# Mixing three phases of a bidirectional scan stage in each step

## The chip, the cores and the metric

The kernel runs on one core of one Trainium2 chip. The metric is device time in microseconds of one execution, as the median of several runs. Beside it there is one profiled execution, with its own time and a span from its first to its last instruction. Lines of the source are named L1034 and so on, as the profile names them. PE is the matrix engine, DVE the vector engine, ACT the scalar engine, POOL is GpSimd, and SP is the queue that issues every DMA of this kernel.

## The reference, cut to what matters

Four residual layers follow one another on an image batch of 32 x 192 channels x 56 x 56, all in float32: an attention layer, a bidirectional recurrence, a shifted small convolution, and a long convolution done by Fourier transforms. Each takes the group norm of its input and adds its result to that input. The change lies in the second layer:

```python
xs = jnp.transpose(x.reshape(B, C, H * W), (0, 2, 1))       # x is the group norm here
k, v, r = xs @ Wk.T, xs @ Wv.T, xs @ Wr.T
x_fwd = wkv_scan(real_w, u, k, v)                            # forward in the token index
x_bwd = flip(wkv_scan(real_w, u, flip(k, 1), flip(v, 1)), 1) # and backward
h = jax.nn.sigmoid(r) * 0.5 * (x_fwd + x_bwd)
h = (h - mean(h)) * rsqrt(var(h) + LN_EPS) * ln_g + ln_b     # layer norm over the channels
out = h @ Wo.T                                               # added to the layer's input
```

One scan keeps two running sums with a decay, one of exp(k) v and one of exp(k), and gives at each token (sum with a bonus u for the token itself) / (the same for the denominator). Tokens are the 3136 pixels of an image. A backward sum at a token needs every later token's k and v, so the backward scan of an image can only start when the forward pass over that image has computed k and v for its last chunk.

## The kernel before, in words

`scan_pairs` takes the images in 16 pairs. Channels lie on partitions: a pair needs three tiles, two of 128 channels (one for each image) and one that holds the last 64 channels of both. The 3136 tokens are cut in NM = 4 chunks of MC = 784, so everything of a chunk is three tiles of 128 x 784 float32 (`t` = 0, 1, 2). Tiles 0 and 1 go through PE together (`pairs.outer`, L835 and L838), tile 2 by itself (`pairs.inner`, L845 and L848).

For each pair the kernel has, in this order in the source:

- the forward half, for chunk 0 to 3: load x, normalize it on ACT to a new tile `xn` (L1016), matmuls with Wk and Wv, exp of k on ACT to `ek` (L1064), `bv` = v times `ek` on DVE (L1069), then for each tile the function `scan`: two scans on DVE (L1034), each with two one-element copies on POOL that carry the running sum in and out (L1029, L1035), and a scalar_tensor_tensor each (L1036). ACT inverts the denominator by a logarithm and an exponential (L1041, L1042), DVE multiplies (L1076) to `y`. `ek`, `bv` and `y` of all four chunks stay in SBUF.
- `stats_for(p + 1)`: all four chunks of the next pair are loaded, measured by bn_stats (L961), and `norm` makes the group norm's scale, which takes two small groups of matmuls (L977, L978 and the helper's lines) with DVE and ACT work between.
- the backward half, for chunk 3 to 0: load x again and normalize it, matmul with Wr, the sigmoid as three ACT passes to `g` (L1095, L1099, L1100), the same `scan` in reverse, and y = (y + backward) times g (L1103 to L1105). At once, for the same chunk, the layer norm and projection: matmul with a centring matrix, squares on ACT to `sq` (L1115), the mean of the squares and the projection on PE, log and exp to `rd` (L1131, L1132), and on DVE rd times the projection (L1133), the residual add onto the loaded x (L1134), bn_stats of the result, and four stores to DRAM (L1138).
- the group norm of the result, whose scale the next layer uses, and a guard that looks at the largest values (`seen`, L1148).

The order on each engine is not that of the source: a scheduler places instructions by what is ready in its own model, and by which tile slots are free. Pools have a fixed number of slots for each name: 6 for `x`, 12 for `ek`, for `bv` and for `y`, 12 together for the working tiles (`xn`, `g`, `sq`, `rd`), 5 for the scans' `p` and `q`, and 4 PSUM tiles of two banks[...]. An instruction that needs a slot waits until the last reader of the slot's former tile is done. Each engine and SP's queue works off its own list in order.

Of the kernel before, what the change touches and what calls it, by code (L numbers as in the profile page):

```python
# [30 lines left out]
S = 56  # L31
# [820 lines left out]
def scan_pairs(ctx: ExitStack, tc: tile.TileContext, a, k, x1, x2, rs2, wogT, count):  # L852
# [9 lines left out]
    wp = ctx.enter_context(tc.tile_pool(name="s_w", bufs=12))  # L862
# [12 lines left out]
    def parts(t):  # L875
        return [t[:, h * HM : (h + 1) * HM] for h in range(2)]
# [76 lines left out]
    def load(p, m):  # L953
        xs = [wp.tile([128, MC], F32, name="x", tag="x", bufs=6) for _ in range(3)]
        for r, t, ap in views(p, m):
            nc.sync.dma_start(out=xs[t][r], in_=ap)
        return xs
# [5 lines left out]
    def new_stats(name):  # L963
        return sp.tile([128, 3, 2 * NM, 6], F32, name=name, tag=name)

    def norm(st):
# [5 lines left out]
        mean = sp.tile([128, 3], F32, name="mean", tag="mean")  # L972
        d = sp.tile([128, 3], F32, name="d", tag="d")
        for step in range(2):
# [12 lines left out]
            else:  # L987
                rs = sp.tile([128, 3], F32, name="rs", tag="rs")
# [4 lines left out]
        nb = sp.tile([128, 3], F32, name="nb", tag="nb")  # L993
# [3 lines left out]
    def stats_for(p):  # L997
        st = new_stats("st1")
        for m in range(NM):
            for t, x in enumerate(load(p, m)):  # L1000
                stats_of(st, m, t, x)
        return norm(st)

    nxt = stats_for(0)
    for p in range(NB // 2):
        _, rs, nb = nxt
        seen = sp.tile([128, 5, 3 * NM], F32, name="seen", tag="seen")
        ek = [[kp.tile([128, MC], F32, name="ek", tag="ek") for _ in range(3)] for _ in range(NM)]
        bv = [[kp.tile([128, MC], F32, name="bv", tag="bv") for _ in range(3)] for _ in range(NM)]
        y = [[kp.tile([128, MC], F32, name="y", tag="y") for _ in range(3)] for _ in range(NM)]  # L1010

        def normed(m, rs=rs, nb=nb, p=p):
            xs = load(p, m)
            xn = [wp.tile([128, MC], F32, name="xn", tag="t") for _ in range(3)]
            for t in range(3):
                nc.scalar.activation(xn[t], xs[t], AF.Identity, bias=nb[:, t : t + 1], scale=rs[:, t : t + 1])  # L1016
            return xs, [parts(t) for t in xn]

        def scan(m, t, carry, rev):

            b, e = bv[m][t], ek[m][t]
            c = eu[:, of(t)]
            got = []
            for i, src in enumerate((b, e)):
                s = wp.tile([128, MC + 1], F32, name="pq"[i], tag="pq", bufs=5)
                edge, last = (MC, 0) if rev else (0, MC)
                out, before = (s[:, 0:MC], s[:, 1:]) if rev else (s[:, 1:], s[:, 0:MC])
                at = carry[t][i]
                nc.gpsimd.tensor_copy(s[:, edge : edge + 1], at)  # L1029
                if rev:  # L1030
                    out, data = out[:, ::-1], src[:, ::-1]
                else:
                    data = src[:, :]
                nc.vector.tensor_tensor_scan(out, decay[:, of(t)].to_broadcast([128, MC]), data, at, ALU.mult, ALU.add)  # L1034
                nc.gpsimd.tensor_copy(at, s[:, last : last + 1])  # L1035
                nc.vector.scalar_tensor_tensor(before, src, c, before, ALU.mult, ALU.add)  # L1036
                got.append(before)
            return got

        def inverse(den, m, t, which, seen=seen):  # L1040
            nc.scalar.activation(den, den, AF.Ln)  # L1041
            nc.scalar.activation(den, den, AF.Exp, scale=-1.0, accum_out=seen[:, which, 3 * m + t : 3 * m + t + 1])  # L1042

        def start():
            carry = [[sp.tile([128, 1], F32, name=f"c{i}{t}", tag=f"c{i}{t}") for i in range(2)] for t in range(3)]
            for c in carry:
                for s in c:
                    nc.gpsimd.memset(s, 0.0)  # L1048
            return carry


        carry = start()
        for m in range(NM):
            _, xn = normed(m)
            for tiles in ((0, 1), (2,)):
                for wt in (wk, wv):
                    ps = [turned() for _ in tiles]
                    if len(tiles) == 2:
                        pairs.outer(wt, [s[2] for s in ps], xn)
                    else:  # L1060
                        pairs.inner(wt, ps[0][2], xn)
                    for t, (_, both, _) in zip(tiles, ps):
                        if wt is wk:
                            nc.scalar.activation(  # L1064
                                ek[m][t].rearrange("p (h n) -> p h n", h=2), both, AF.Exp,
                                accum_out=seen[:, 0, 3 * m + t : 3 * m + t + 1],
                            )
                        else:
                            nc.vector.tensor_tensor(  # L1069
                                bv[m][t].rearrange("p (h n) -> p h n", h=2), both,  # L1070
                                ek[m][t].rearrange("p (h n) -> p h n", h=2), ALU.mult,
                            )
                for t in tiles:
                    num, den = scan(m, t, carry, False)
                    inverse(den, m, t, 1)
                    nc.vector.tensor_tensor(y[m][t], num, den, ALU.mult)  # L1076

        if p + 1 < NB // 2:
            nxt = stats_for(p + 1)


        carry = start()
        st2 = new_stats("st2")
        for m in reversed(range(NM)):
            xs, xn = normed(m)
            h = y[m]
            for tiles in ((0, 1), (2,)):
                ps = [turned() for _ in tiles]
                if len(tiles) == 2:
                    pairs.outer(wr, [s[2] for s in ps], xn)  # L1090
                else:
                    pairs.inner(wr, ps[0][2], xn)
                for t, (_, both, _) in zip(tiles, ps):
                    g = wp.tile([128, MC], F32, name="g", tag="t")
                    nc.scalar.activation(  # L1095
                        g.rearrange("p (h n) -> p h n", h=2), both, AF.Exp, scale=-1.0,
                        accum_out=seen[:, 3, 3 * m + t : 3 * m + t + 1],
                    )
                    nc.scalar.activation(g, g, AF.Ln, bias=1.0)  # L1099
                    nc.scalar.activation(g, g, AF.Exp, scale=-1.0)  # L1100
                    num, den = scan(m, t, carry, True)
                    inverse(den, m, t, 2)
                    nc.vector.tensor_tensor(num, num, den, ALU.mult)  # L1103
                    nc.vector.tensor_tensor(h[t], h[t], num, ALU.add)
                    nc.vector.tensor_tensor(h[t], h[t], g, ALU.mult)  # L1105
            hs = [parts(t) for t in h]
            sq = [wp.tile([128, MC], F32, name="sq", tag="t") for _ in range(3)]
            for tiles in ((0, 1), (2,)):
                ps = [turned() for _ in tiles]
                if len(tiles) == 2:  # L1110
                    pairs.outer(centre, [s[2] for s in ps], hs)
                else:
                    pairs.inner(centre, ps[0][2], hs)
                for t, (_, both, _) in zip(tiles, ps):
                    nc.scalar.activation(  # L1115
                        sq[t].rearrange("p (h n) -> p h n", h=2), both, AF.Square,
                        accum_out=seen[:, 4, 3 * m + t : 3 * m + t + 1],
                    )
            sqs = [parts(t) for t in sq]
            for tiles in ((0, 1), (2,)):  # L1120
                pv, po = [turned() for _ in tiles], [turned() for _ in tiles]
                if len(tiles) == 2:
                    pairs.outer(mean_w, [s[2] for s in pv], sqs)
                    pairs.outer(wog, [s[2] for s in po], hs)
                else:
                    pairs.inner(mean_w, pv[0][2], sqs)
                    pairs.inner(wog, po[0][2], hs)
                for t, (_, var, _), (_, out, _) in zip(tiles, pv, po):
                    rd = wp.tile([128, MC], F32, name="rd", tag="t")
                    rdh = rd.rearrange("p (h n) -> p h n", h=2)  # L1130
# [6 lines left out]
            for r, t, i, c in places:  # L1137
                nc.sync.dma_start(out=x2[c, i, rows, p], in_=xs[t][r].rearrange("p (h w) -> p h w", w=S))  # L1138
# [567 lines left out]
```

## Time and profile before

| what | us |
|---|---|
| median of 3 runs (14577.73 to 14602.56) | 14596.81 |
| profiled execution, its own time | 14588.21 |
| its span | 14586.4 |
| scan stage within the span, 5402 to 9976 | 4574 |
| DVE busy in that stage | 3717.5 |
| PE busy in that stage | 3308.6 |
| ACT busy in that stage | 2132.1 |
| one pair, 5959.0 to 6240.5 | 281.5 |

The profile's first part gives the busy time of each engine over the whole span, in which the attention stage comes ahead of the scans (to about 5400) and the two convolutions behind them (from about 9976). Averages over the span therefore mix three stages. Busy time by stage, the list of who waited for whom, and the timeline of single instructions are asked for each stage apart. In a timeline line the first number is the start, the second the duration, and the bracket at the end gives the idle time of the engine just before, with the instruction that ended it.

### The profile page before, as it was taken

To read this page: it belongs to the slowest core of one execution; us is meant where nothing else is said; L and a number is where in the kernel's file an instruction comes from. 1 tells how busy PE (TensorE), PEld (TensorE's weight loads), DVE (VectorE), ACT (ScalarE), POOL (GpSimd) and SP (SyncE) were. 2 spreads that over 40 slices of the span, in tenths; PEclk is the share of its full clock that TensorE was granted. 3 is DMA by queue.
4 is the path that set the end of the run, shared out by engine and by line. 5 is a ranking of instruction groups with operands and counts; after the bars stand their busy time and mean duration, and the time that the engine had idled before them with its cause. 6 is when DMAs were issued, how large, how long until landed. Compare 5 with 4: busy or idle time off the path is not lost. (4 is left out here: it accounts for less than half of the span.)

```text
span 14586.4 us, 164705 instructions
## 1 busy us (share of the span) xinstructions
PE 12276.2 (84%) x63542; PEld 7620.1 (52%) x63542; DVE 11320.3 (78%) x15929; ACT 5972.2 (41%) x10826; POOL 2178.7 (15%) x2238
## 2 busy tenths in 40 slices
PE   4999999999999976777677677767899889988898
PEld 2655655655565553333333333335666666666666
DVE  4878877887887878878887887886777777777777
ACT  2444444444444434444444444443323232323323
POOL 0000000000000004434443443442000000000000
PEclk8999999999999988888888888888999999999999
DMA  2001001000100112232223222322111111111111
GB/s 54 27 27 40 27 27 40 27 27 32 35 27 27 40 53 66 60 71 71 65 67 81 66 60 68 75 51 56 35 37 36 37 37 36 37 35 38 36 37 23
DMA packets 886784, 654.14 MB, mean 45 GB/s; under 512 B 764942, under 2 KB 772857, under 8 KB 876976
## 3 DMA queue, kind: packets, MB, share of 16 engines
q1 hardware_dynamic: 885992, 643.51, 16.7%
q8 instruction: 505, 8.27, 0.2%
q14 instruction: 287, 2.35, 0.1%
HBM read 402.88 MB, written 240.50 MB: 44 GB/s over the span
## 5 line engine op out<-in xcount | busy, mean ns | idle before, releaser
L587 DVE SCALAR_TENSOR_TENSOR o<-v_a,dww,o 128x896 f32<-128x896 f32 (+1 forms) x1024 | 1052.8, 1028 | 390.1 <-ACT v_a L561 282.7
L1633 ACT COPY y<-ps 64x252 f32<-64x252 f32 (+1 forms) x2376 | 807.6, 340 | 1298.6 <-PE ps L1627 1266.4
L1567 PE MATMUL ps<-f,imag 84*84 84x112 f32 x6144 | 1032.0, 261 | 130.2 <-DVE imag L1560 128.5
L1574 ACT COPY z<-ps 84x448 f32<-84x448 f32 x768 | 405.3, 528 | 1771.1 <-PE ps L1567 1771.1
L1567 PE MATMUL ps<-f,real 84*84 84x112 f32 x6144 | 1035.7, 261 | 1.7
L1567 PEld LDWEIGHTS ps<-f,imag 84*84 84x84 f32 x6144 | 744.0, 153 | 275.6 <-DVE imag L1560 206.4
L1567 PEld LDWEIGHTS ps<-f,real 84*84 84x84 f32 x6144 | 748.8, 153 | 160.1 <-issue 68.6
L1041 ACT ACTIVATE q<-q 128x784 f32<-128x784 f32 x384 | 329.3, 858 | 1225.4 <-DVE q L1036 1223.9
L1035 POOL COPY c<-p 128x1 f32<-128x1 f32 x384 | 696.2, 1813 | 665.3 <-DVE p L1034 611.8
L1048 POOL MEMSET c<- 128x1 f32 x192 | 18.3, 99 | 5182.8 <-PE ps L719 5172.1
L1034 DVE TENSOR_TENSOR_SCAN q<-decay,c,ek 128x784 f32<-128x784 f32 x384 | 702.0, 1832 | 105.3 <-ACT ek L1064 105.2
L1583 PE MATMUL ps<-z,f 84*114 84x448 f32 x1536 | 658.5, 551 | 129.5 <-ACT z L1574 129.5
L604 ACT ACTIVATE pr<-ps,low 98x896 f32<-98x896 f32 (+1 forms) x384 | 350.1, 914 | 1015.4 <-DVE low L602 1015.4
L1585 DVE TENSOR_TENSOR o<-ps,rs 114x448 f32<-114x448 f32 x384 | 239.5, 624 | 631.7 <-PE ps L1583 630.5
L1035 POOL COPY c<-q 128x1 f32<-128x1 f32 x384 | 483.1, 1258 | 1460.7 <-DVE q L1034 1390.3
L1034 DVE TENSOR_TENSOR_SCAN p<-decay,c,bv 128x784 f32<-128x784 f32 x384 | 699.9, 1833 | 0.0
L674 PE MATMUL ps<-gq_a,xs_a 128*112 128x294 f32 x1792 | 643.7, 442 | 0.0
L600 PE MATMUL ps<-xs_a,gk_a 128*98 128x448 f32 (+1 forms) x1536 | 639.0, 497 | 0.0
L587 DVE SCALAR_TENSOR_TENSOR o<-v_c,dww,o 128x448 f32<-128x448 f32 (+1 forms) x1024 | 634.0, 619 | 4.0
L1547 PE MATMUL re<-y,f 128*84 128x420 f32 (+1 forms) x1152 | 561.5, 569 | 84.8 <-ACT y L1633 74.8
L601 PE MATMUL ps<-xs_c,gk_c 125*98 125x448 f32 (+1 forms) x1536 | 631.6, 492 | 0.0
L675 PE MATMUL ps<-gq_c,xs_c 125*112 125x294 f32 x1792 | 627.7, 433 | 0.0
(352 smaller groups left out, 29243.6 us busy)
## 6 DMA issues: line engine op xcount, KB each, us to landing
x<-x SPq DMA_DIRECT2D x512, 392.0 KB
x<-x SPq DMA_DIRECT2D x512, 196.0 KB
x<-x SPq DMA_DIRECT2D x192, 399.0 KB
out_x<-x SPq DMA_DIRECT2D x384, 196.0 KB
x_a<-in_x SPq DMA_DIRECT2D x32, 1568.0 KB
x<-x_a SPq DMA_DIRECT2D x32, 1568.0 KB
x_c<-in_x SPq DMA_DIRECT2D x64, 392.0 KB
x<-x_c SPq DMA_DIRECT2D x64, 392.0 KB
```

The costliest lines, as they stand in the source:

```text
L587: nc.vector.scalar_tensor_tensor(dst, tap(i), dww[:, t, i : i + 1], dst, ALU.mult, ALU.add)
L600: mm(ps[P2, h, :n], g[:, cols], xs_a[j][:, px], start=True, stop=False)
L601: mm(ps[P2, h, :n], gk_c[0:KC, 2 * j + h, cols], xs_c[j][0:KC, px], start=False, stop=True)
L674: mm(ps[:SUB, i, :HA], xs_a[j][:, px], g, start=True, stop=False)
L675: mm(ps[:SUB, i, :HA], xs_c[j][0:KC, px], gq_c[0:KC, 2 * j + (q + i) // ns], start=False, stop=True)
L1034: nc.vector.tensor_tensor_scan(out, decay[:, of(t)].to_broadcast([128, MC]), data, at, ALU.mult, ALU.add)
L1035: nc.gpsimd.tensor_copy(at, s[:, last : last + 1])
L1547: nc.tensor.matmul(ps[:, : n * 84], f2[:, i, :], y[:, i0 : i0 + n].rearrange("p g s u -> p (g s u)"), start=True, stop=True)
L1567: nc.tensor.matmul(ps[:84, i * 2 * S : (i + 1) * 2 * S], part[:, i0 + i].rearrange("p s u -> p (s u)"), f3[:, m, :], start=(m == 0), stop= ...
L1574: nc.scalar.copy(z[:, i0 : i0 + n].rearrange("p g m w -> p (g m w)"), ps[:84, : n * 2 * S])
L1583: nc.tensor.matmul(got, f4[:, m, :], z[:, i0 : i0 + n, m, :], start=(m == 0), stop=(m == 1))
L1633: nc.scalar.copy(y[64 * m : 64 * m + 64, 2 * g0 + i : 2 * (g0 + n) : 2], got[64 * i : 64 * i + 64, :, :, m, :])
```

## The change

The phases become functions, and the loop over pairs is written anew. A pair's data go into a `State`. `forwards(s, m)` is a chunk of the forward half and `backwards(s, m)` the backward sums of a chunk up to y times g. `finish(s, m)` is what came behind them in the same chunk: layer norm, projection, residual, stores. `measure` is the statistics of one chunk, `conclude` the group norm of the result and the guard.

Step i of pair p now holds: backwards of chunk 3 - i of pair p; finish of the chunk that the step before did (in step 0 this is chunk 0 of pair p - 1); forwards of chunk i of pair p + 1; in steps 0 and 1 the measuring of two chunks of pair p + 2; behind step 2 their norm; behind step 1 the group norm of pair p - 1's result. The statistics of pairs 0 and 1 and the forward half of pair 0 come ahead of the loop, the last finish behind it.

`normed` writes the normalized x over the loaded x, and `finish` loads x once more for the residual. Slots: `x` 7 in place of 6, working tiles 8 in place of 12 (no `xn` any more), `y` 16 in place of 12, and 3 or 4 for some small tiles. The decisive parts of the diff:

```diff
-    wp = ctx.enter_context(tc.tile_pool(name="s_w", bufs=12))
+    wp = ctx.enter_context(tc.tile_pool(name="s_w", bufs=8))
...
-        xs = [wp.tile([128, MC], F32, name="x", tag="x", bufs=6) for _ in range(3)]
+        xs = [wp.tile([128, MC], F32, name="x", tag="x", bufs=7) for _ in range(3)]
...
-            xs = load(p, m)
-            xn = [wp.tile([128, MC], F32, name="xn", tag="t") for _ in range(3)]
-            for t in range(3):
-                nc.scalar.activation(xn[t], xs[t], AF.Identity, bias=nb[:, t : t + 1], scale=rs[:, t : t + 1])
-            return xs, [parts(t) for t in xn]
+    def normed(s, m):
+        xs = load(s.p, m)
+        for t in range(3):
+            nc.scalar.activation(xs[t], xs[t], AF.Identity, bias=s.nb[:, t : t + 1], scale=s.rs[:, t : t + 1])
+        return [parts(t) for t in xs]
...
+        s.y[m] = [kp.tile([128, MC], F32, name="y", tag="y", bufs=3 * NM + 4) for _ in range(3)]
...
+    def finish(s, m):
+        h, xs = s.y[m], load(s.p, m)
...
-        if p + 1 < NB // 2:
-            nxt = stats_for(p + 1)
...
+    last = NB // 2
+
+    def measure(st, p, m):
+        for t, x in enumerate(load(p, m)):
+            stats_of(st, m, t, x)
+
+    s, after, before = State(0, norm(stats_for(0))), norm(stats_for(1)), None
+    for m in range(NM):
+        forwards(s, m)
+    for p in range(last):
+        ahead = State(p + 1, after) if p + 1 < last else None
+        st = new_stats("st1")
+        for i in range(NM):
+            m = NM - 1 - i
+            backwards(s, m)
+            if i > 0:
+                finish(s, m + 1)
+            elif before is not None:
+                finish(before, 0)
+            if ahead is not None:
+                forwards(ahead, i)
+            if p + 2 < last:
+                if i < 2:
+                    measure(st, p + 2, 2 * i)
+                    measure(st, p + 2, 2 * i + 1)
+                elif i == 2:
+                    after = norm(st)
+            if i == 1 and before is not None:
+                conclude(before)
+        before, s = s, ahead
+    finish(before, 0)
+    conclude(before)
```

The bodies of `forwards`, `backwards`, `finish` and `conclude` are those of the old halves, with the names of the `State`.

## The prediction

> **What bounds the kernel now.** I read the page first, then the busy time by stage, then VectorE's (DVE's) waits in the scan stage, then the timelines around a pair's end.
>
> ```profile
> PE 12276.2 (84%) x63542; PEld 7620.1 (52%) x63542; DVE 11320.3 (78%) x15929; ACT 5972.2 (41%) x10826; POOL 2178.7 (15%) x2238
> ```
>
> ```profile
> 5402.00:9976.00 4574.00, 3308.57 (x11650) 1537.11 (x11650) 3717.54 (x4170) 2132.06 (x3523) 1850.51 (x1712) 0.84 0.28 68
> 5959.00:6240.50 281.50, 205.86 (x722) 95.63 (x723) 229.56 (x257) 132.04 (x219) 116.00 (x108) 0.84 0.27 68
> ```
>
> The first is the page's line of the whole span; below it the scan stage and one pair of it (busy us of PE, PEld, DVE, ACT, POOL, then PE's clock, the DMA share, GB/s). The page would name PE as the bound; in this stage it is DVE, 229.6 of 281.5 us a pair, and nothing else passes 206. So 52 us a pair are DVE's gaps. Its waits in the stage:
>
> ```profile
> DVE rd L1133 <- PE ps L838: 340.8, 32, 14.7
> DVE y L1105 <- ACT g L1100: 166.4, 64, 5.1
> DVE q L1034 <- ACT ek L1064: 105.2, 16, 8.9
> DVE seen L1148 <- ACT sq L1115: 99.8, 16, 6.9
> DVE rs L989 <- PE ps L848: 85.4, 32, 3.1
> ```
>
> Columns: us in total, times, longest. The counts say where: 16 is once a pair. The forward half waits only for its first `ek`; the rest lies in the backward half and at the pair's end. One such end:
>
> ```profile
> 5964.48 1.86 DVE L1105 TENSOR_TENSOR y<-y,g 128x784 f32<-128x784 f32 x2 [5.13 <-ACT g L1100]
> 5967.80 0.98 DVE L1105 TENSOR_TENSOR y<-y,g 128x784 f32<-128x784 f32 x1 [1.38 <-ACT g L1100]
> 5974.40 0.17 DVE L1148 TENSOR_SCALAR seen<-seen 128x12 f32<-128x12 f32 x1 [5.62 <-ACT sq L1115]
> 5982.20 1.85 DVE L1133 TENSOR_TENSOR rd<-ps,rd 128x784 f32<-128x784 f32 x2 [7.38 <-PE ps L838]
> 5993.22 0.16 DVE L981 COPY mean<-ps 128x2 f32<-128x2 f32 x1 [1.52 <-PE ps L848]
> 5997.25 0.16 DVE L989 TENSOR_SCALAR rs<-ps 128x2 f32<-128x2 f32 x1 [3.11 <-PE ps L848]
> 5997.98 0.16 DVE L994 SCALAR_TENSOR_TENSOR nb<-mean,rs 128x3 f32<-128x3 f32 x1 [0.51 <-ACT rs L992]
> 6004.58 3.59 DVE L1034 TENSOR_TENSOR_SCAN q<-decay,c,ek 128x784 f32<-128x784 f32 x2 [6.31 <-ACT ek L1064]
> ```
>
> The brackets add to 31.0 us of idle in one pass: last chunk's layer norm, group norm, first `ek` of the next pair, one after another with no scan to fill them.
>
> **What the skill says.** "Perfetto Trace Analysis" (Optimization Strategy) advises interleaving regimes whose most-contended engine differs; the counts above agree that there is something to interleave. "PSUM — Partial Sum Buffer" (Engine vs sequencer instructions): the ACT, DVE and POOL queues are strict first-in-first-out, and matmuls start in program order; so a mixed order can still wait behind a late instruction. "TensorE: Matmul & The Clock Gate" (What's actually happening): PE falls to half clock after about 3.4 us idle and needs as long to recover. The trace agrees in kind:
>
> ```profile
> 6111.72 0.56 PE L977 MATMUL ps<-d,grp_aa 128*128 128x1 f32 x2 [5.22 <-DVE d L985]
> ...
> 6114.57 5.59 PE L835 MATMUL ps<-xn,Wr_aa 128*128 128x392 f32 x8
> 6120.09 1.91 PE L838 MATMUL ps<-xn,Wr_ca 64*128 64x392 f32 x8
> ```
>
> From `d` the group-norm matmuls take 2.85 us and the pair of Wr tiles 7.4, where warm ones (mean_aa 2.90, mean_ca 1.59) take 4.5.
>
> **The parts, costed.** Nothing is removed from DVE, ACT, PE or POOL; added are one load of x per chunk and nothing else. Loads go from 12 to 16 tile triples a pair: 14.4 MB to 19.3, with the stores' 4.8 some 24 MB in 256 us = 94 GB/s. At the stage's start the same loads ran at 256 GB/s, so bandwidth is covered; 16 more issues at 0.33 us on SP are 5 us a pair, hidden.
>
> *DVE's step.* From timeline start-to-start distances a scan takes 1.75 us, a scalar_tensor_tensor 0.94, a tensor_tensor 0.88, a bn_stats 0.47. Backward of a chunk (6 scans, 6 stt, 9 tt) is 24.1 us, finish (3 tt, 3 stt, 6 bn) 8.4, forward (6, 6, 6) 21.5: 54.0 a step, 216 a pair, plus 24 bn of measuring (11.4) and small ones: 229, the busy time above. That is the floor.
>
> *What still waits.* The built order of the changed program shows, per engine, the sequence below; I followed each of a pair's four steps through the in-order queues, with durations of the profile (ACT: ln 0.75, exp with sum 0.84, g or sq 0.80, x norm 0.93; PE: a pair of tiles 4.5 warm, a third tile 3.1). Zero is the first backward scan.
>
> Step 0 (chunk 3, finish of the predecessor's chunk 0): wog is done at 20.2, DVE comes to `rd` at 25.0: no wait. Step 1: wog 24.5, DVE 26.9: none; one bn_stats waits 0.7 for an x tile whose slot a store has to leave.
>
> Step 2: the group norm of the finished pair stands on PE ahead of Wr. `d` leaves DVE at 3.3, matmuls to 6.3 (DVE waits 1.4 at `rs`), Wr pair cold to 13.7. ACT then runs g, the q inverses and g's log and exp without a gap from 13.8 to 24.0, and only then sq. From sq to the pair of `rd` is mean 4.5 + wog 4.5: 33.9. DVE, with its backward done, arrives at 27.5: **6.4 us** wait, and 0.7 for the third tile.
>
> Then the new wait. In steps 2 and 3 the x norm of the next backward stands on ACT ahead of `ek`, and its load needs the slot of the tile that finish has just stored. The store and the reuse of its slot, the load and its reader:
>
> ```profile
> 6733.11 1.32 SPq L1138 DMA_DIRECT2D x<-x  x2
> 6737.08 0.33 SPq L956 DMA_DIRECT2D x<-x  x1
> ...
> 6842.02 1.85 SPq L956 DMA_DIRECT2D x<-x  x1
> ...
> 6847.20 1.04 ACT L1016 ACTIVATE xn<-x,nb,rs 128x784 f32<-128x784 f32 x1 [2.59 <-DMA x<-x]
> ```
>
> Store to slot 3.4 to 4.0 us, load 3.3 after its issue ends (about 2.9 by the fit in "DMA: Bandwidth & Descriptors", Anatomy of one DMA; that fit is for another issuing path, and I use the trace's number). So 7.2 from the end of the first residual add, norm 0.9, `ek` 0.9: 9.0, plus a hop. DVE's cover is the rest of finish, 5.6 us, and PE's Wk pair comes in at about the same time: DVE waits **2.8** before the forward scan. Behind that norm on ACT stand `ek` and the q inverses; who waits is only DVE's scan. The loads behind the stores on SP are for the later backward half and land in time.
>
> Step 3: the measuring norm, likewise: `d` at 5.6, `rs` wait 2.0, inverse waits 0.5; ACT takes g only after the second q logarithm (17.4), sq ends 29.2, PE gives wog at 36.6, DVE arrives at 28.5: **8.1**; third tile 0.6; `ek` 2.7.
>
> Sum: 0.7 + 11.3 + 13.9 = 26 us a pair in place of 52; a pair is 229.5 + 26 = 256. An extreme of 0 is DVE alone; an extreme of all of the old 14.7-us chain in every step is rival C.
>
> *POOL.* The edge copies stay in their number. In the old trace DVE never waits for POOL; in the new order each edge copy stands at least one scan ahead of its reader. I take 0; if a slot of the five p/q tiles comes late, 1.8 us (one copy, L1035) a step, 7 a pair.
>
> *Ends.* Statistics of pair 1 now stand ahead of the first scan: 12 more tiles at about 1.5 us (5405 to 5422 in the old trace for 12), partly instead of later work and with the first `ek` behind it: +14. Before, first scan (5437.8) to the last group norm (9964) is 4526. After: forward of pair 0 alone 89; 15 pairs of 256 = 3840, less 8.4 (no predecessor) and 11.4 (no pair to measure); pair 15 without a forward 130 busy + about 27 idle; its last finish 35 (chain 14.7, 8.4, norm 12). Sum 4101. Change: 4101 + 14 - 4526 = **-411 us**. On the profiled execution's 14588.2 that is 14177; on the median shown, 14596.8, it is **14186**.
>
> **Rivals.**
> A: DVE packs almost fully, idle 8 a pair: ACT or PE run ahead more than my walk allows. For it: the four PSUM tiles and ACT's 47% load leave room. Against: the sq-after-g order is fixed in the queue. 14186 - 15 x 18 = 13916.
> B: the chain is late in steps 0 and 1 too, where my slack is 5 and 2.4 us, through semaphore hops or cold matmuls: idle 43. 14186 + 15 x 17 = 14441.
> C, slower: the in-order queues reproduce the old worst wait at `rd` (14.7 us, as in the second fence's longest) in each of four steps, with norms 3.4 and `ek` 5.5 beside it: idle 68, 14186 + 15 x 42 = 14816. It decides from 53 us a pair, 13 a step, since 411/15 = 27 above my 26. Against it: finish works on the chunk of the step before, so its centre matmuls need nothing of the current scans; for it: nothing but the FIFO rule.
> That the change does not mix is excluded: in the built order every pair's forward scans stand between the predecessor's backward ones.
>
> **Numbers.** Forecast 0.55, A 0.17, B 0.19, C 0.07, about the same (no difference that counts) 0.02. The forecast's own range is idle 17 to 35 a pair: 14050 to 14320. For 8 in 10 I go into A and B: 13950 (idle 10) to 14440 (idle 43). Below 0.2% of the time, 29 us, this kernel's measurement does not tell a change. Faster 0.91, same 0.02, slower 0.07.
>
> **What would show it.** Right: DVE about 90% busy in the middle of the stage; `seen` and most `y` waits gone; waits of `rd` about twice a pair at 6 to 8 us; `rs` twice a pair at 1 to 2; and the forward q scan's wait for `ek` twice a pair near 3, with ACT's x norm waiting for DMA just before it. PE's clock above 0.84. Wrong: DVE waiting for POOL, or for DMA at bn_stats by more than 1 us; `rd` waits four times a pair; a gap in the first 100 us much above 14.

## The result, and the profile after

The changed kernel takes 14180.4 us (median of 4 runs, 14167.8 to 14187.8), the kernel before in the same session 14593.2 (14577.7 to 14602.6). The ratio is 0.9716, 95% interval 0.9704 to 0.9728: faster by 2.8%, 413 us. The forecast was 14186. Its profiled execution took 14187.84 us, with a span of 14185.5.

The page's line of the whole span, changed kernel (busy us, share, instructions):

```profile
PE 12164.8 (86%) x63542; PEld 7571.3 (53%) x63542; DVE 11327.6 (80%) x15929; ACT 5948.9 (42%) x10826; POOL 2153.5 (15%) x2238
```

The instruction counts of all engines and DVE's busy time (11320.3 before) are what they were. The span is shorter, and PE is busy 111 us less for the same instructions. The busy time by stretch (same columns as before: length; PE, PEld, DVE, ACT, POOL; PE's clock, DMA share, GB/s): 13 whole pairs of the changed kernel, then 13 whole pairs of the kernel before. A pair is counted from one `fine` mark to the next; that instruction ends the guard and comes once a pair.

```profile
5815.94:9172.24 3356.30, 2582.45 (x9460) 1204.46 (x9456) 3019.80 (x3367) 1711.34 (x2860) 1469.04 (x1398) 0.87 0.38 94
5693.02:9387.62 3694.60, 2689.59 (x9465) 1249.20 (x9465) 3015.70 (x3367) 1731.89 (x2860) 1499.99 (x1404) 0.84 0.28 69
```

A pair takes 258.2 us, of which DVE is busy 232.3 and idle 25.9; before, it took 284.2, with DVE busy 232.0 and idle 52.2. (The single pair shown for the kernel before, 281.5 with DVE busy 229.6, is a little shorter than this mean.) PE's clock stands at 0.87, 0.84 before.

What DVE waits for in the stage now (us in total, times, longest):

```profile
DVE rd L1132 <- PE ps L838: 197.8, 30, 10.8
DVE q L1035 <- ACT ek L1066: 96.3, 30, 8.3
DVE rs L989 <- PE ps L848: 60.6, 32, 3.1
```

`y <- g` (166.4 before) and `seen <- sq` (99.8 before) are gone but for one wait each. `rd` is down from 340.8 to 197.8, about twice a pair. `ek` now counts twice a pair where it was once. One pair on DVE's timeline, steps 2 and 3; in brackets the idle time ahead of each instruction and who ended it:

```profile
6956.94 0.16 DVE L989 TENSOR_SCALAR rs<-ps 128x2 f32<-128x2 f32 x1 [1.35 <-PE ps L848]
6983.84 1.86 DVE L1132 TENSOR_TENSOR rd<-ps,rd 128x784 f32<-128x784 f32 x2 [5.85 <-PE ps L838]
...
6996.56 3.59 DVE L1035 TENSOR_TENSOR_SCAN q<-decay,f,ek 128x784 f32<-128x784 f32 x2 [3.63 <-ACT ek L1066]
7025.98 0.16 DVE L989 TENSOR_SCALAR rs<-ps 128x2 f32<-128x2 f32 x1 [2.16 <-PE ps L848]
7053.35 1.86 DVE L1132 TENSOR_TENSOR rd<-ps,rd 128x784 f32<-128x784 f32 x2 [7.37 <-PE ps L838]
...
7065.40 3.60 DVE L1035 TENSOR_TENSOR_SCAN q<-decay,f,ek 128x784 f32<-128x784 f32 x2 [2.96 <-ACT ek L1066]
```

Nearly all that is left lies in steps 2 and 3, the steps behind a group norm. PE's timeline of step 2 shows what stands ahead of `rd` there:

```profile
6953.97 0.56 PE L977 MATMUL ps<-d,grp_aa 128*128 128x1 f32 x2 [18.16 <-DVE d L985]
...
6956.82 5.59 PE L835 MATMUL ps<-x,Wr_aa 128*128 128x392 f32 x8
...
6966.84 2.90 PE L835 MATMUL ps<-y,cen_aa 128*128 128x392 f32 x8
...
6974.97 2.90 PE L835 MATMUL ps<-sq,mean_aa 128*128 128x392 f32 x8 [0.73 <-ACT sq L1114]
...
6982.15 1.59 PE L838 MATMUL ps<-y,wog_ca 64*128 64x392 f32 x8
```

PE stands still for 18.16 us in front of the group norm's second half, because DVE comes to `d` only behind its forward scans. Wr and the centre matmuls (`cen`) are queued behind it, then the mean of the squares and the projection (`wog`). From `d` on PE runs almost without a gap: 30 us to `rd`, and DVE has only 22.7 us of other work in that time. By the Trainium skill ("PSUM — Partial Sum Buffer", Engine vs sequencer instructions) matmuls start in program order, and the trace agrees. How long the norm alone holds Wr is another question, since Wr also needs the last normalized x tile. The two steps differ in that, step 2 first:

```profile
6954.29 1.04 ACT L1017 ACTIVATE x<-x,nb,rs 128x784 f32<-128x784 f32 x1 [5.56 <-DMA x<-x]
```

```profile
7010.03 1.04 ACT L1017 ACTIVATE x<-x,nb,rs 128x784 f32<-128x784 f32 x1 [3.76 <-DMA x<-x]
7023.02 0.56 PE L977 MATMUL ps<-d,grp_aa 128*128 128x1 f32 x2 [16.89 <-DVE d L985]
7025.87 5.20 PE L835 MATMUL ps<-x,Wr_aa 128*128 128x392 f32 x8
```

In step 3 that tile is ready at 7011.1 and Wr starts at 7025.9: the norm holds Wr for 14.8 us. In step 2 the tile waits for its load and is ready at 6955.3, only 1.5 us before Wr starts; there the load is nearly as late as the norm.

The first Wr group is cold, 5.59 us for eight records where the warm centre group takes 2.90; that agrees with the skill's "TensorE: Matmul & The Clock Gate" (What's actually happening), since 18 us of idle went before it. That page has about 3.4 us for the way back to the full clock; here the eight records are slow for 5.5 us, after 2.85 us of the norm's own matmuls.

The second kind of wait on the timelines of ACT and of SP, the end of step 2:

```profile
6994.69 1.04 ACT L1017 ACTIVATE x<-x,nb,rs 128x784 f32<-128x784 f32 x1 [6.12 <-DMA x<-x]
6995.64 0.80 ACT L1066 ACTIVATE ek<-ps 128x784 f32<-128x784 f32 x1
```

```profile
6986.66 1.32 SPq L1137 DMA_DIRECT2D x<-x  x2
6990.64 0.33 SPq L956 DMA_DIRECT2D x<-x  x1
```

The two stores of tile 0 go out at 6986.66. The load for the next backward half has to wait for that slot, 3.98 us, and then lands 4.05 us after its issue, where ACT's x norm waits for it; `ek` stands behind that norm, and DVE's forward scan behind `ek`.

### The profile page after: what moved, and what is told of

Its sections match the earlier page's. It is cut to its first block, busy times and chain, and to the rows that moved or that the text cites. A ratio compares the mean times of both kernels' runs of the same rounds, so it can differ in the third digit from the quotient of the medians.

```text
span 14185.5 us, 165124 instructions
## 1 busy us (share of the span) xinstructions
PE 12164.8 (86%) x63542; PEld 7571.3 (53%) x63542; DVE 11327.6 (80%) x15929; ACT 5948.9 (42%) x10826; POOL 2153.5 (15%) x2238
## 5 line engine op out<-in xcount | busy, mean ns | idle before, releaser
L1480 POOL TENSOR_TENSOR mat<-tap,tap 114x114 f32<-114x114 f32 x96 | 40.9, 426 | 3790.9 <-PE ps L1538 2256.7
L1591 DVE TENSOR_TENSOR a<-re,g 84x420 f32<-84x420 f32 (+1 forms) x576 | 353.7, 614 | 245.2 <-PE re L1584 245.2
L1584 PE MATMUL im<-y,f 128*84 128x420 f32 (+1 forms) x1152 | 528.1, 540 | 0.0
L1664 PE MATMUL ps<-f,padded 114*128 114x168 f32 x3168 | 517.9, 319 | 11.4 <-issue 7.8
```

What stands on the lines that cost most here:

```text
L1584: nc.tensor.matmul(ps[:, : n * 84], f2[:, i, :], y[:, i0 : i0 + n].rearrange("p g s u -> p (g s u)"), start=True, stop=True)
L1591: nc.vector.tensor_tensor(a0, f[0], gr.to_broadcast(shape), ALU.mult)
L1664: nc.tensor.matmul(ps[:, g * 168 : (g + 1) * 168], flat[:, (g0 + g) * 128 : (g0 + g + 1) * 128], f1, start=True, stop=True)
```

## The experiments

They come in three groups: the reasons for the 25.9 us that are left; which half of the change brings the gain; the price of the added load, with checks on the readings before. The table sums them up. Each ratio is to runs of the kernel before beside it, whose medians lay between 14599.1 and 14600.0. "Idle" is DVE's idle time between 6100 and 9000 us of each kernel's profile, 2900 us in the middle of the stage (stretches that aren't whole pairs, so good to some us a pair).

| kernel | median us | ratio to before, 95% | DVE idle in 2900 us |
|---|---|---|---|
| before | 14599.8 | 1 | 526 |
| changed kernel, again | 14180.7 | 0.9713 (0.9700–0.9726) | 286 |
| group norms spread | 14081.4 | 0.9645 (0.9632–0.9658) | 221 |
| nine x tiles | 14122.1 | 0.9676 (0.9663–0.9690) | 256 |
| both | 14008.3 | 0.9592 (0.9578–0.9605) | 171 |
| mixed, layer norm in its own step | 14829.4 | 1.0166 (1.0149–1.0183) | 616 |
| not mixed, layer norm one step late | 14184.2 | 0.9724 (0.9708–0.9741) | 295 |
| changed, sq first | 14132.5 | 0.9689 (0.9672–0.9705) | 265 |
| all edits | 13864.3 | 0.9498 (0.9482–0.9514) | 60 |
| before, second load alone | 14581.1 | 0.9989 (0.9982–0.9995) | 515 |
| measuring in steps 2 and 3 | 14131.0 | 0.9679 (0.9663–0.9695) | 259 |
| not mixed, sq first, nine x tiles | 14247.8 | 0.9760 (0.9744–0.9777) | 336 |
| mixed, sq first, nine x tiles | 14106.7 | 0.9662 (0.9646–0.9678) | 238 |

### Why the rest is idle

The changed kernel itself, as the base:

> The changed kernel itself, as the base for the three variants beside it: 14180 us on the medians so far, within 0.2%; in the scan stage about 7 us of `rd` wait twice a pair, 1.3 to 2.2 us of `rs` wait twice a pair, about 3.2 us of `ek` wait twice a pair.

It came at 14180.7, so the three beside it can be set against it.

**The norms out of Wr's way.** `norm` becomes a generator, and `forwards` takes its parts at fixed places:

```diff
+    def norm_parts(st):
         ...
+        yield
         for step in range(2):
             ...
             pairs.inner(group, [ps[:, 1, 2:3]], [[s] for s in src])
+            yield
         ...
+        yield
         nc.vector.scalar_tensor_tensor(nb, mean, -1.0, rs, ALU.mult, ALU.mult)
+        yield mean, rs, nb
     ...
+    def forwards(s, m, side=None):
         ...
         for tiles in ((0, 1), (2,)):
+            if side is not None and len(tiles) == 2:
+                next(side)
             for wt in (wk, wv):
                 ...
+            if side is not None:
+                next(side)
             for t in tiles:
                 ...
+        return None if side is None else next(side)
```

So bn_aggr comes ahead of Wk, the means' matmuls behind Wv of tiles 0 and 1, `d` and its matmuls behind Wv of tile 2; a further `next` in `scan`, behind the first sum of tile 2, takes `rs`. The norms are the same two, in the same steps.

> Both group norms are spread through the forward half of their step instead of standing at its end, so that their matmuls on PE come before and just behind the third tile's Wv and no longer hold Wr until DVE has reached `d`. My theory (the norm ahead of Wr is what makes `rs` and `rd` late): the `rs` waits go (3.5 us a pair). In step 3 the Wr pair could start at the end of the last x norm, some 13 us earlier, so its `rd` wait of 7.4 goes too. In step 2 that x norm itself waits for its load (it ended at 6955.2 where Wr started at 6956.8), so only 1 to 2 of 5.9 us go there. About 12 us a pair, 14 pairs: 170 us less than the changed kernel, 14010. Rival (`rd` is late because ACT takes sq only behind all of g and the q inverses, and those wait for DVE's scans, wherever Wr starts): only the `rs` waits go, 50 us, 14130, and `rd` still waits 5 to 7 us in both steps.

Measured: 14081.4, 99 us less than the changed kernel, between the two. DVE's waits in the 2900 us:

```profile
DVE rs L994 <- PE ps L848: 51.9, 24, 2.2
DVE rd L1145 <- PE ps L838: 36.0, 11, 3.9
```

In the same stretch of the changed kernel `rd` had 140.0 us in 22 waits. Of two `rd` waits a pair one is gone, and the other fell from 7.37 to 3.87 us. In step 3, where the norm alone held Wr, moving it took 3.5 us off the wait. In step 2 the cause is not separated: the edit moved the load too. The last x norm ahead of Wr now ends 9.7 us before Wr starts, where it was 1.5, and by the trace of the changed kernel Wr could have started only those 1.5 us earlier with the norm alone out of its way. (Nine x tiles alone, the next run, leave both waits, 5.68 and 7.37 us.) Two things came otherwise than I expected. It is step 2's wait that went and step 3's that stayed, not the other way. And `rs` was not helped: each still waits 2.2 us, since the built order put it one instruction behind `d`, and PE's group norm takes that long from `d` wherever it stands.

**More x tiles.**

```diff
-    wp = ctx.enter_context(tc.tile_pool(name="s_w", bufs=8))
+    wp = ctx.enter_context(tc.tile_pool(name="s_w", bufs=6))
-        xs = [wp.tile([128, MC], F32, name="x", tag="x", bufs=7) for _ in range(3)]
+        xs = [wp.tile([128, MC], F32, name="x", tag="x", bufs=9) for _ in range(3)]
```

> Nine x tiles in place of seven (paid for with six instead of eight work tiles), so that the load for the next backward half no longer needs the slot of a tile that finish has just stored. My theory (store, slot, load, x norm on ACT ahead of `ek`): the `ek` waits of 3.6 and 3.0 us shrink by what the x norm is later than PE's Wk pair, 1.5 us or more each, at most to nothing: 3 to 6 us a pair, 14090 to 14135. Rival (PE's Wk pair is as late as the x norm, because it stands behind the wog that made `rd` late): `ek` still waits 3 us twice a pair and the time is that of the changed kernel, 14180, within 0.1%. In both, `rd` and `rs` stay as they are.

Measured: 14122.1, 59 us less. ACT's `ek` is now released by PE:

```profile
6972.47 0.82 ACT L1066 ACTIVATE ek<-ps 128x784 f32<-128x784 f32 x1 [5.51 <-PE ps L838]
```

```profile
DVE q L1035 <- ACT ek L1066: 46.1, 22, 2.1
```

No wait of `ek` is longer than 2.1 now, where they were 3.63 and 2.96. The waits of bn_stats for DMA (9.8 us in this stretch) are gone too. So both theories were partly right: the chain from store to load to x norm set the last 0.9 to 1.5 us of each wait, and behind it Wk, which PE takes behind the late wog, sets the other 2.1.

**Both edits.**

> Both edits together. My theory: with the norms out of Wr's way and the load for the next backward half no longer behind measuring or a store, Wr starts early in both steps, and all of 26 us of waits a pair but some 4 to 8 go: 20 us a pair, 14 pairs, 280 us: 13900, not below 13860 (DVE alone without waits). Rival (the ACT queue's order bounds `rd`): 14080 to 14130, with `rd` still at 5 to 7 us twice a pair.

Measured: 14008.3, between my number and the rival's, and 172 us less than the changed kernel; the two gains (99 and 59) add, and perhaps a little more. What is left:

```profile
DVE rs L994 <- PE ps L848: 52.0, 24, 2.2
DVE q L1041 <- ACT ek L1076: 49.8, 24, 2.1
DVE rd L1145 <- PE ps L838: 49.2, 21, 3.9
```

`rd` waits 2.3 us on average; here ACT's order shows at last: the third tile's sq stood behind a q logarithm that waited 2.39 us for DVE.

### Which half of the change brings the gain

**Mixed, but the layer norm in its own step.**

```diff
             backwards(s, m)
-            if i > 0:
-                finish(s, m + 1)
-            elif before is not None:
-                finish(before, 0)
+            finish(s, m)
             if ahead is not None:
                 forwards(ahead, i)
```

(and no `finish` behind the loop.)

> Half of the change undone: the next pair's forward sums stay mixed in, but each chunk's layer norm comes in the step of its own backward sums, as before the change. In the built order of DVE `rd` still stands ahead of the step's forward scans. My theory (the delay of the layer norm by one step is what hides its chain; the forward scans cannot, they stand behind `rd` in DVE's queue): cen, sq, mean and wog lie open after every backward half, some 10 us in each of four steps, less where bn_stats fill them: 66 us idle a pair, 14600 to 14800, no faster than the kernel before, `rd` waits four times a pair. Rival (the mixing of two pairs is what brings the gain): 14200 to 14350.

Measured: 14829.4, 1.7% slower than the kernel before and a little above my range. DVE's waits in the 2900 us (about ten pairs):

```profile
DVE rd L1132 <- PE ps L838: 206.9, 33, 13.6
DVE st L961 <- DMA x<-x: 203.4, 66, 4.4
```

The second line I had not foreseen: measuring's bn_stats wait for their loads some six times a pair, as much again as `rd`. But these waits are not a second cause. They stand in the two steps that measure, just ahead of `rd`:

```profile
6844.24 1.04 DVE L961 BATCH_NORM_STATS2 st<-x 128x6 f32<-128x392 f32 x2 [4.28 <-DMA x<-x]
6848.36 1.04 DVE L961 BATCH_NORM_STATS2 st<-x 128x6 f32<-128x392 f32 x2 [3.09 <-DMA x<-x]
6852.53 1.04 DVE L961 BATCH_NORM_STATS2 st<-x 128x6 f32<-128x392 f32 x2 [2.72 <-DMA x<-x]
6854.76 1.86 DVE L1132 TENSOR_TENSOR rd<-ps,rd 128x784 f32<-128x784 f32 x2 [0.79 <-PE ps L838]
```

`rd` still has to wait for PE behind them: with every load in time DVE would have stood at `rd` instead. So the chain from cen to wog is open in all four steps, up to 13.6 us, and DVE waits for `ek` in each of them (39 times in the stretch). What sets the late loads themselves was not tested.

**Not mixed, but the layer norm one step late.**

```diff
-            if ahead is not None:
-                forwards(ahead, i)
     for p in range(last):
+        s = State(p, after)
+        for m in range(NM):
+            forwards(s, m)
+            if m == 0 and before is not None:
+                finish(before, 0)
+        if before is not None:
+            conclude(before)
+        if p + 1 < last:
+            after = norm(stats_for(p + 1))
         for i in range(NM):
             m = NM - 1 - i
             backwards(s, m)
             if i > 0:
                 finish(s, m + 1)
```

> The other half undone: pairs are not mixed, each runs its four forward chunks, then the next pair's measuring, then its four backward chunks; but the layer norm is one step late, and that of the last chunk comes behind the first forward chunk of the next pair. My theory: without forward scans a step still has 24 us of backward work to hide wog, which my walk put at 20 to 24.5 us behind the step's start, so most of the gain remains: idle 20 to 30 us a pair, 14080 to 14250. Rival (the forward scans are needed, because g and the layer norm of a step take more of ACT and PE than 32 us of DVE hide): waits of `y` for g and of `rd` in every backward step, idle 40 or more, 14380 to 14500.

Measured: 14184.2, the time of the changed kernel, and 258.4 us a pair from mark to mark where that has 258.2. The delay by one step alone brings all of the gain; mixing alone makes the kernel slower; mixing on top of the delay adds nothing that shows. Its waits are others, though:

```profile
DVE rd L1132 <- PE ps L838: 163.3, 22, 9.1
DVE q L1035 <- ACT ek L1066: 54.8, 22, 4.5
```

Here `rd` waits at the seam between two pairs, 9.0 us in the last backward step and 8.3 behind the first forward chunk; in the steps between there is no such wait. In the changed kernel the seam is closed, and the waits of steps 2 and 3 cost about the same.

**sq ahead of the backward half.**

```diff
-    def finish(s, m):
-        h, xs = s.y[m], load(s.p, m)
+    def squares(s, m):
+        h = s.y[m]
         hs = [parts(t) for t in h]
         ...
-        sqs = [parts(t) for t in sq]
+        return h, hs, [parts(t) for t in sq]
+
+    def finish(s, m, got):
+        (h, hs, sqs), xs = got, load(s.p, m)
         ...
+            of_chunk = (s, m + 1) if i > 0 else (before, 0)
+            got = squares(*of_chunk) if of_chunk[0] is not None else None
             backwards(s, m)
-            if i > 0:
-                finish(s, m + 1)
-            elif before is not None:
-                finish(before, 0)
+            if got is not None:
+                finish(*of_chunk, got)
```

> The changed kernel with one edit: the centre matmuls and sq of the delayed layer norm are issued ahead of the backward half of the step, so that sq no longer stands behind g and the q inverses on ACT; the group norms stay where they were. My theory after the first four runs: from `d` on PE runs its queue almost without a gap (norm 2.9, Wr 10, cen 7.4, mean and wog of two tiles 8.9: 29 us of the 30 until `rd`), so the order on ACT costs only PE's two gaps before mean, 0.7 and 1.6 us: 30 us less than the changed kernel, 14150. Rival (the ACT order as my prediction had it): sq some 8 us earlier, most of both `rd` waits gone, 14030 to 14070.

Measured: 14132.5, by the two ratios some 35 to 50 us less than the changed kernel, nearer to my number than to the rival's, but not for my reason. The waits:

```profile
DVE y L1101 <- ACT g L1096: 89.4, 44, 2.3
...
DVE rd L1135 <- ACT rd L1134: 43.8, 19, 2.3
...
DVE rd L1135 <- PE ps L838: 7.3, 3, 2.5
```

`rd` fell from 140 to 51 us, as the rival had it; but now Wr stands behind the centre matmuls, g is late, and `y` waits four times a pair. That one of the two has to be late as long as the norm holds PE is my reading of this; no run shows it apart.

**All edits.** Norms spread, with the reading of the second mean put behind the first scans of the next backward half; nine x tiles; sq first; pair 1 measured between the chunks of the first forward pass:

```diff
-    def backwards(s, m):
+    def backwards(s, m, side=None):
     ...
-                num, den = scan(s, m, t, s.back, True)
+                num, den = scan(s, m, t, s.back, True, side if t == 0 else None)
     ...
-    s, after, before = State(0, norm(stats_for(0))), norm(stats_for(1)), None
+    s, st, before = State(0, norm(stats_for(0))), new_stats("st1"), None
     for m in range(NM):
-        forwards(s, m)
+        side = norm_parts(st) if m == 3 else None
+        forwards(s, m, side)
+        for n in ((0, 1), (2,), (3,), ())[m]:
+            measure(st, 1, n)
+    after = list(side)[-1]
```

> Norms spread through the forward half, with the reading of the second mean put behind the first scans of the next step's backward half; nine x tiles; centre and sq ahead of the backward half; and pair 1 measured during the first forward pass instead of ahead of it. My theory: what is left in the run with both first edits (rs 4.3, ek 4.2, rd 4.7, p 0.7 us a pair: 14 us) goes nearly all, since PE is then ahead by the 2 us that it lacked, and the start gives back some 10 us: 14008 - 14 x 14 - 10 = 13800; half of it would be 13900. Rival (PE or ACT are by then as full as DVE, so that other waits take their place): 13950 to 14010.

Measured: 13864.3, 5.0% faster than the kernel before and 2.2% faster than the changed one. The time lies between my 13800 and the 13900 for half of it, but the waits are nearly gone:

```profile
DVE q L1041 <- ACT ek L1076: 29.2, 15, 2.1
DVE rd L1147 <- PE ps L838: 9.8, 12, 0.8
```

```profile
6100.00:9000.00 2900.00, 2440.31 (x8983) 1136.62 (x8982) 2839.56 (x3176) 1625.62 (x2708) 1340.18 (x1319) 0.91 0.40 102
```

`rs` is out of the list, and DVE is busy for 98% of the stretch. This stage is now within 2% of DVE's own work. Whether the unmixed kernel could be brought there too was not run.

### The added load, and two checks

**The second load alone, in the kernel before.**

```diff
-            xn = [wp.tile([128, MC], F32, name="xn", tag="t") for _ in range(3)]
             for t in range(3):
-                nc.scalar.activation(xn[t], xs[t], AF.Identity, bias=nb[:, t : t + 1], scale=rs[:, t : t + 1])
-            return xs, [parts(t) for t in xn]
+                nc.scalar.activation(xs[t], xs[t], AF.Identity, bias=nb[:, t : t + 1], scale=rs[:, t : t + 1])
+            return xs, [parts(t) for t in xs]
     ...
-            hs = [parts(t) for t in h]
+            xs, hs = load(p, m), [parts(t) for t in h]
```

(and seven x tiles, eight work tiles.)

> The kernel before with one part of the change alone: x is normalised in its own tile and loaded a second time for the residual (seven x tiles and eight work tiles, as in the changed kernel); nothing is mixed or delayed. My theory (the added loads are hidden, bandwidth and issue are covered): the time of the kernel before within 0.2%, 14570 to 14630. Rival (in a queue of stores and loads on seven slots the second load comes late, some 3 us in each of four chunks a pair): 14790, with `x` of the residual add waiting for DMA.

Measured: 14581.1, ratio 0.9989 (0.9982 to 0.9995). The DMA rate in the 2900 us rises from 68 to 85 GB/s, and the kernel isn't slower; if anything it is 0.1% faster. So in the kernel before the price of the added load is nothing, as the prediction had it. In the changed kernel it was not taken out by itself; there the loads' slots do cost something, as nine x tiles showed (59 us).

**Measuring moved.**

```diff
-                if i < 2:
-                    measure(st, p + 2, 2 * i)
-                    measure(st, p + 2, 2 * i + 1)
-                elif i == 2:
+                if i >= 2:
+                    measure(st, p + 2, 2 * i - 4)
+                    measure(st, p + 2, 2 * i - 3)
+                if i == 3:
                     after = norm(st)
```

> The changed kernel with the next pair but one measured in steps 2 and 3 instead of 0 and 1, its norm at the end of step 3; the other norm stays at the end of step 1. My theory (`rd` is late in the step behind a norm): long `rd` waits in steps 2 and 0, still twice a pair, none in step 3; 14120 to 14240. Rival (`rd` is late in steps 2 and 3 because these have no 5.7 us of bn_stats to cover it): the waits move to steps 0 and 1, none in step 2 or 3, the same time.

Measured: 14131.0, within my range and some 50 us less than the changed kernel. A long `rd` wait stands once a pair only, in step 0, behind the norm that was moved there:

```profile
6794.40 0.16 DVE L989 TENSOR_SCALAR rs<-ps 128x2 f32<-128x2 f32 x1 [2.16 <-PE ps L848]
...
6820.82 1.86 DVE L1132 TENSOR_TENSOR rd<-ps,rd 128x784 f32<-128x784 f32 x2 [5.63 <-PE ps L838]
```

The wait followed its norm out of step 3 into step 0, and step 1, which lost its bn_stats, didn't get one: that speaks against the rival. But step 2, still behind a norm, has no `rd` wait, against my theory: there bn_stats now lie ahead of `rd`, waiting for DMA themselves (71.5 us in the stretch, up to 4.0). In the pair shown wog is done at 6942.8, while DVE stands 5.3 us for loads and comes to `rd` at 6944.9; I estimate from this that without the load waits it would have been at `rd` about 3 us too early. So wog is late in the step behind a norm, and other work or other waits of DVE can cover it.

**Both orders with equal edits.** sq first and nine x tiles, on the unmixed kernel and on the changed one:

> The unmixed kernel with the late layer norm, and two edits more: centre and sq ahead of the backward half, nine x tiles. Its two open seams, `rd` 9.0 and 8.3 us a pair, came from sq standing behind g or the forward q inverses on ACT: with sq ahead they go for the most part, and `ek` 3.5 shrinks to 2: 18 us a pair, 13930. If the seams were PE's and not ACT's, 14100.

> The changed kernel (pairs mixed) with the same two edits, centre and sq ahead of the backward half and nine x tiles, norms where they were: the counterpart of the run before it. From the runs with one edit each, 48 and 59 us less than 14180: 14070 if they add. If mixing pays once the layer norm is out of the way, it is below the unmixed one; my theory is that it isn't, since the norms' hold on Wr remains here: 50 to 150 us above the unmixed one.

Measured: 14247.8 unmixed, 64 us slower than without the two edits, and 14106.7 mixed. Both expectations failed, mine on the order of the two among them. Which of the two edits did the harm in the unmixed kernel was not run apart; its waits point to sq:

```profile
DVE y L1101 <- ACT g L1096: 121.9, 22, 9.6
...
DVE seen L1153 <- ACT sq L1114: 57.2, 11, 6.3
```

At its seam the last backward half has only itself to work on. With sq first, g is late in place of sq, by up to 9.6 us, and nothing covers it. In the mixed kernel the longest such wait of `y` is 4.4. Here mixing is worth 141 us. So the statement that mixing adds nothing holds for the two kernels with `finish` undivided, and no further.

## Why the prediction was right, step by step

- *DVE's floor, 229.5 us a pair:* measured 232.3, the mean of 13 pairs. It was 2.8 short, since it was checked against one pair that is shorter than the mean (232.0 in the kernel before as well).
- *Idle 26 us a pair:* measured 25.9. Step by step in the pair shown, predicted and measured: bn_stats 0.7 and 0.67; `rs` 1.4 and 1.35, then 2.0 and 2.16; `rd` 6.4 and 5.85, then 8.1 and 7.37; third tile 0.7 and 0.6 against 0.35 each; `ek` 2.8 and 3.63, then 2.7 and 2.96. No wait of `rd` in steps 0 and 1, as the walk had it.
- *From the first scan to the last norm, 4101 us:* measured 4093 (5468.0 to 9560.6). That this is only 8 off is in part luck. The walk gave all 15 pairs their 26 us of waits, but the first has no norm ahead of its step 2, and the last but one of the 16 has none ahead of its step 3; that makes up for most of what the floor lacked (15 pairs of 256 less 20 are 3820, measured 3830). The last pair with its finish took 177 in place of 192, the first forward pass 86 in place of 89.
- *The start, +14 us:* from the stage's first DVE instruction to the first scan 53.7 us where it was 35.7, so +18. Right in kind, 4 short.
- *POOL 0, bandwidth covered:* no wait for POOL in the list; 94 GB/s where 94 was worked out; the load alone measured at 0.9989 in the kernel before.
- *The signs it named:* those of being right came: DVE 90% busy in the middle of the stage (2614 of 2900 us), `rd` and `ek` twice a pair, PE's clock at 0.87. Of those of being wrong one came in part: bn_stats waited for DMA by up to 2.1 us, over the 1 us named, but only 15.2 us in the whole stage.
- *The mechanism of `rd`:* the first part, the norm ahead of Wr, holds for step 3, where the norm held Wr for 14.8 us and moving it took 3.5 us off the wait; in step 2 the walk left out that Wr's own x tile came only 1.5 us before the norm was done. The second part, that ACT's order makes the time between Wr and sq, was given too much weight: PE's own queue filled that time (gaps of only 0.73 and 1.58 us ahead of mean), and with sq moved forward the wait went over to g. The walk came to the right sum because both queues take about equally long.
- *The mechanism of `ek`:* both halves were there, as the walk said; the runs put the store and load at 0.9 to 1.5 us of it and Wk at 2.1.
- *What it left out:* it took the change as one piece. Rival C's picture, the chain open in every step, worked out at 14816; the kernel with mixing and without the delay measured 14829. The mechanism agrees, a chain open in four steps; that the number agrees so closely is chance, since C's chain was the old 14.7 us each time and this one is shorter, with more of `ek` beside it. What keeps the change from that end is the delay of the layer norm, not the mixing that its name puts first.

## What to carry to other kernels

Where an engine's gaps come from a chain that its own last result starts, put that chain one step behind, on data that is ready; do this first and alone, since mixing without it can be slower than nothing (14829 here), and on top of it may add nothing at all (14180 and 14184). Then look in each in-order queue for a short instruction that waits for a late result (a group norm's matmul here): its price can be not its own 2.9 us but the time by which it holds all that stands behind it, 14.8 us in step 3. Ask what else those instructions wait for, though, before you put it all down to the one ahead. A freed wait can go over to the next in the queue, as from `rd` to `g` here, so such an edit can cost where nothing covers the new wait (the unmixed kernel, 14248 after 14184).

## What the runs showed of the hardware

In the kernel before, loading 4.8 MB more a pair through the same queue, a third more than it loaded, cost no time at all (0.9989), with the DMA engines' share at 0.34. And the one-column matmuls of a group norm, fourteen records, take PE 2.85 us after a long gap (18.16 us here). DVE waits 1.35 to 2.17 us for `rs` where one instruction stands between `d` and `rs` in the pairs shown, and 3.11 in the kernel before, where none does: short products are no cheap step on a path.
